# Splitting an attention block's end over three engines, and a bias as an extra weight row

## The chip, the cores and the metric

The kernel runs on one core of one Trainium2 chip, alone. The metric is the device time of one execution in microseconds (us), the median of several. A core has five engines with a queue of instructions each, which run in parallel and wait for each other by semaphores: TensorE (PE; weight loads are listed apart as PEld), VectorE (DVE), ScalarE (ACT), GpSimd (POOL) and SyncE (SP), which here only issues DMA transfers. Matmul results land in PSUM, everything else on the core lies in SBUF. All data is float32, and a float32 matmul appears in the trace as two matmul instructions.

## The reference

For each of four images x of 256 channels by 64 x 64 pixels (N = 4096 pixels), a self-attention layer is followed by a clustering layer with an MLP. The first one:

```python
q = einsum('oc,bcn->bno', wq, xf) + bq          # 32 channels
k = einsum('oc,bcn->bon', wk, xf) + bk[None, :, None]
attn = softmax(einsum('bnd,bdm->bnm', q, k), axis=-1)   # 4096 x 4096
v = einsum('oc,bcn->bon', wv, xf) + bv[None, :, None]
out = einsum('bcn,bmn->bcm', v, attn)
x = gamma[0] * out + x
```

The second layer, cut to what matters here, with the group norms taken over all channels and pixels of an image:

```python
y = x + ls1 * cluster(group_norm(x), ...)        # ends in conv1x1(out, proj_w, proj_b)
h = gelu(conv1x1(group_norm(y), mlp_w1, mlp_b1)) # 1024 channels
y = y + ls2 * conv1x1(h, mlp_w2, mlp_b2)
z = relu(batch_norm(y * dw_w)); out = relu(batch_norm(conv1x1(z, pw_w)))
```

## The kernel before, in words

The images are worked on one after the other, each in three stages: `attention`, `cluster`, `mlp`. An image lies in SBUF as four tiles of 1024 pixels (`xs`), is overwritten in place by the attention's result, and the next image's tiles are loaded while `mlp` frees them.

**Attention.** The 4096 query pixels are cut into 8 blocks of 512 (`nb`), the 4096 key pixels into 8 groups of 512 (`g`), so there are 64 units `u = 8*nb + g`. For one unit, `score` computes four 128x512 pieces of scores into two PSUM tiles (`sc`, halves of 128x1024; the pool `ps_s` has two such buffers, so the next unit's score can only start when both halves have been read), ScalarE copies them to an SBUF slot `s` (L282, L287; 10 slots), and VectorE keeps a running maximum `top` (L286, L289). After a block's eighth score, `fold` and `across` find the maximum of each query, and `spread` brings it into PSUM as `mb` by a matmul (L314). `exps` subtracts it on VectorE (L326), takes the exponential on ScalarE (L329) and sums on GpSimd into `acc` (L331 for the first group, then twice L334 a group; one `acc` buffer, so that the next block's first sum waits for the reading of the old one). `weigh` multiplies the exponentials with v into `av`, two PSUM tiles (L339, 16 matmul instructions a unit).

The scores run 9 units ahead of `weigh` (LEAD). The first nine scores are mixed with the computation of v (`v_pair`, L241; copies out of PSUM on VectorE and ScalarE in turn, L251 and L249). At a block's last unit, `finish` copies `av` times gamma into two tiles `t` (ScalarE L350, VectorE L351), computes the sum of the exponentials by matmuls with a matrix of ones (`den`, L354), takes its reciprocal (L356), multiplies (L358), adds gamma times v's bias and x (L360) and takes the statistics that the next group norm needs (bn_stats, L363).

**The order.** The program is written as above, and a scheduler then orders each engine's instructions by what they need. All 16 subtractions of a block, for example, come early in the block, as soon as `mb` is there, with the two maxima of each newer score between them. On the chip each engine takes its queue in this order.

**Cluster** starts with `group_norm` (bn_aggr of the statistics, two small matmuls with `mean_w`, square root, reciprocal), then projects, normalizes (L504: squares on GpSimd), finds for every pixel the best of four centers, and forms `gp`, the projected center values, by one matmul with `wproj_s` (96 rows) and one more that adds the projection bias by a row `row16` and `projb` (L600, L603). **MLP** runs per block of 512 pixels: 8 hidden tiles `hs` from the shared buffers with tag "w", the last convolution, and a DMA of the result.

At the start of the program, SP issues the loads in order; at most eight are under way, so that each later issue waits for the load eight before it. `projb` is made by a small matmul (L165) from `pc_s`.

## Time and profile before

| What | Value |
|---|---|
| Time, median of 3 | 4210.15 us (4208.2 to 4210.23) |
| Profiled execution, its own time | 4209.54 us |
| Its span | 4207.7 us |
| First score matmul | 38.98 us |
| First image: attention's blocks from den to den (block 0 to 6) | 156.11 to 639.87 us |
| First image: `den` of block 7 begins, bn_aggr begins | 696.51, 705.74 us |
| Granted TensorE clock, mean | 0.929 |

A page of the profile gives each engine's busy time and share, the chain of work that ended last (followed back from the last instruction), and groups of equal instructions with busy time, mean duration and the idle time of the engine just before them. An arrow `<-` names who ended a wait. "issue" is time in which nothing that the profile shows was waited for. Over the 40 slices of the span, TensorE and VectorE are busy like this (tenths):

```profile
PE   8998998799999899889999989988999989998899
...
DVE  4557655400456765540055675643005576564300
```

### The profile page before, as it was taken

The page shows a single profiled execution, that of the slowest core. Times are in us where ns is not written, and L with a number is a line of the kernel's source. Part 1 is how long each engine was busy: PE and PEld are TensorE (multiplying, and loading weights), DVE is VectorE, ACT ScalarE, POOL GpSimd, SP SyncE. Part 2 cuts the span into 40 slices and gives each one's busy share as a digit, 9 for nine tenths or more (in the row PEclk, how much of TensorE's full clock was granted, in tenths as well). Part 3 has the DMA queues.
Part 4 walks back from the last instruction along what each step waited for, and adds up shares of the span by engine and source line. Part 5 has one row for each costly group of instructions (what it writes and reads, how often), then busy time and mean ns, then how long its engine had stood idle before and what let it go on. Part 6 is the DMA issues. An engine that isn't in the chain of part 4 may idle for free.

```text
span 4207.7 us, 28649 instructions
## 1 busy us (share of the span) xinstructions
PE 3864.4 (92%) x11176; PEld 1736.7 (41%) x11176; DVE 1950.2 (46%) x1982; ACT 1471.3 (35%) x1723; POOL 1202.3 (29%) x526
## 2 busy tenths in 40 slices
PE   8998998799999899889999989988999989998899
PEld 4333334544433333444443333344444333335444
DVE  4557655400456765540055675643005576564300
ACT  5434432122634443212263443411226344341122
POOL 1534533000143553300024454340003345343000
PEclk9999999699999999969999999996999999998799
DMA  2000000010000000001000000000100000000000
GB/s 75 1 0 0 0 0 0 1 38 28 15 1 0 0 0 0 0 1 40 25 16 0 0 0 0 0 1 5 35 25 16 0 0 0 0 0 1 5 15 20
DMA packets 17639, 38.99 MB, mean 9 GB/s; under 512 B 2688, under 2 KB 4832, under 8 KB 17504
## 3 DMA queue, kind: packets, MB, share of 16 engines
q1 hardware_dynamic: 17504, 37.16, 2.5%
q8 instruction: 88, 1.44, 0.1%
q14 instruction: 47, 0.39, 0.0%
HBM read 20.38 MB, written 16.78 MB: 9 GB/s over the span
## 4 chain that ended last, share of the span: by engine, by line
PE 81%; DVE 16%; issue 2%; ACT 1%; DMA 0%; SPq 0%; DVEq 0%; ACTq 0%
PE av L339 37%; PE h L682 11%; PE mo L671 10%; PE sc L276 7%; DVE s L326 3%; DVE x L360 3%; PE pw L709 3%; PE vp L241 3%; DVE rden L356 2%; DVE t L358 2%; PE qp L256 2%; PE kp L220 1%; PE dots L510 1%; PE fp L436 1%; PE vp L448 1%
## 5 line engine op out<-in xcount | busy, mean ns | idle before, releaser
L339 PE MATMUL av<-s,v 128*128 128x512 f32 x4096 | 1877.7, 612 | 0.0
L339 PEld LDWEIGHTS av<-s,v 128*128 128x128 f32 x4096 | 780.7, 196 | 1076.4 <-issue 1054.2
L334 POOL TENSOR_TENSOR acc<-acc,s 128x1024 f32<-128x1024 f32 x448 | 1090.6, 2434 | 163.8 <-ACT s L329 130.8
L331 POOL TENSOR_TENSOR acc<-s 128x1024 f32<-128x1024 f32 x32 | 75.5, 2360 | 2207.6 <-ACT s L329 1168.5
L329 ACT ACTIVATE s<-s 128x1024 f32<-128x1024 f32 x512 | 532.0, 1056 | 444.6 <-DVE s L326 430.1
L326 DVE TENSOR_TENSOR s<-s,mb 128x1024 f32<-128x1024 f32 x512 | 591.1, 1210 | 36.2 <-PE mb L314 36.2
L286 DVE TENSOR_TENSOR top<-sc,top 128x1024 f32<-128x1024 f32 x224 | 272.1, 1215 | 677.4 <-PE sc L276 677.4
L276 PE MATMUL sc<-q,k 32*128 32x512 f32 x2048 | 356.2, 666 | 178.0 <-DVE top L289 171.2
L282 ACT COPY s<-sc 128x1024 f32<-128x1024 f32 x256 | 258.0, 1008 | 681.6 <-PE sc L276 681.6
L682 PE MATMUL h<-xn,w_s 128*128 128x512 f32 x1024 | 488.1, 601 | 8.3 <-DVE xn L656 6.2
L671 PE MATMUL mo<-hs,w_s 128*128 128x512 f32 x1024 | 476.1, 593 | 0.0
L698 DVE SCALAR_TENSOR_TENSOR x<-mo,pc_s,x 128x512 f32<-128x512 f32 x64 | 48.0, 751 | 918.5 <-PE mo L671 915.1
L690 ACT ACTIVATE hs<-h,pv_s 128x512 f32<-128x512 f32 x256 | 175.9, 687 | 579.2 <-PE h L682 577.0
L287 ACT COPY s<-sc 128x1024 f32<-128x1024 f32 x256 | 258.5, 1010 | 135.2 <-DVE top L286 93.6
L682 PEld LDWEIGHTS h<-xn,w_s 128*128 128x128 f32 x1024 | 197.5, 193 | 255.2 <-issue 253.2
L671 PEld LDWEIGHTS mo<-hs,w_s 128*128 128x128 f32 x1024 | 194.9, 190 | 244.8 <-issue 244.8
L289 DVE TENSOR_TENSOR top<-sc,top 128x1024 f32<-128x1024 f32 x224 | 273.4, 1220 | 17.9 <-DVE top L286 0.5
L276 PEld LDWEIGHTS sc<-q,k 32*128 32x128 f32 x2048 | 95.4, 190 | 384.8 <-DVE top L289 191.1
L360 DVE SCALAR_TENSOR_TENSOR x<-t,gbv,x 128x512 f32<-128x512 f32 x64 | 161.6, 2564 | 0.0
L709 PE MATMUL pw<-z,wpw_s 128*128 128x512 f32 x256 | 118.7, 607 | 3.3 <-ACT z L702 3.3
L241 PE MATMUL vp<-wv_s,x 128*128 128x256 f32 x512 | 119.1, 386 | 0.0
L284 DVE TENSOR_TENSOR top<-sc,s 128x1024 f32<-128x1024 f32 x32 | 39.2, 1224 | 158.6 <-ACT s L282 158.6
(143 smaller groups left out, 1972.8 us busy)
## 6 DMA issues: line engine op xcount, KB each, us to landing
x<-in_x SPq DMA_DIRECT2D x32, 512.0 KB, 4.8
out<-o SPq DMA_DIRECT2D x64, 256.0 KB, 2.0
w_s<-in_w SPq DMA_DIRECT2D x2, 1024.0 KB, 6.8
cst<-in_consts SPq DMA_DIRECT2D x1, 338.0 KB, 7.4
wqk_l<-in_wqk SPq DMA_DIRECT2D x1, 256.0 KB, 2.7
wv_s<-in_wv SPq DMA_DIRECT2D x1, 256.0 KB, 10.0
wpw_s<-in_wpw SPq DMA_DIRECT2D x1, 256.0 KB, 8.1
wfv_s<-in_wfv SPq DMA_DIRECT2D x1, 192.0 KB, 6.6
```

The lines of the kernel that those rows point to most:

```text
L276: nc.tensor.matmul(halves[r // 2][:, r % 2, :], k_s[rows, g, :], q_s[rows, :], start=True, stop=True)
L282: nc.scalar.copy(s[:, 0:2, :], halves[0])
L286: nc.vector.tensor_tensor(top, halves[1], top, ALU.max)
L287: nc.scalar.copy(s[:, 2:4, :], halves[1])
L289: nc.vector.tensor_tensor(top, halves[0], top, ALU.max)
L326: nc.vector.tensor_tensor(sh, sh, mxs[nb].unsqueeze(1).to_broadcast([P, 2, NB]), ALU.subtract)
L329: nc.scalar.activation(sh, sh, AF.Exp)
L334: nc.gpsimd.tensor_tensor(acc, acc, s[:, 2 * h : 2 * h + 2], ALU.add)
L339: nc.tensor.matmul(av[c], v_t[:, RG * g + quarter, c * P : (c + 1) * P], slots[u][:, quarter, :], start=(g == 0 and quarter == 0), stop=(g ...
L360: nc.vector.scalar_tensor_tensor(yb, ts[c], gbv[:, c : c + 1], yb, ALU.add, ALU.add)
L671: nc.tensor.matmul(acc[c], w2_s[:, j, c * P : (c + 1) * P], hs[j], start=(j == 0), stop=(j == HID // P - 1),)
L682: nc.tensor.matmul(ps[:, 0, :], w1_s[:, k, j * P : (j + 1) * P], xn[:, k, :], start=(k == 0), stop=(k == KC - 1),)
```

## The change: what it does

- **The block's end.** GpSimd first adds the two halves of `acc`, so `den` is one matmul. ScalarE copies `den` into SBUF. The reciprocal is taken there in four pieces of 128 columns, one in each of the next block's units 1 to 4, between `weigh`'s quarters. At unit 5, GpSimd multiplies both halves of `t` by it (128x1024) and adds them into x (128x1024). Unit 6 has nothing, and at unit 7 VectorE takes the statistics. After the last block the pieces run one after the other.
- **v's bias** is no longer added at the block's end. It is loaded into all partitions, and GpSimd adds it to v after ScalarE's copies (all of them now on ScalarE).
- **Projection bias:** `wproj_s` has a 97th row, loaded by a DMA of single values, and `agg` a 97th row with the ones; the second matmul of `gp`, `row16`, `projb` and the matmul that made it are gone.
- **Smaller:** `mean_w` is replaced by `ones` and a factor 1/128; the tag "w" has four buffers instead of five, shared by `dg`.

```diff
-    bv_s = loaded("bv_s", bv.rearrange("(k p o) -> p k o", p=P, o=1), [P, KC, 1])
+    bv_s = loaded("bv_s", bv.partition_broadcast(P), [P, C])
...
-    wproj_s = loaded("wproj_s", wproj, [ED, C])
+
+    wproj_s = const.tile([ED + 1, C], F32, name="wproj_s")
+    nc.sync.dma_start(out=wproj_s[:ED], in_=wproj)
+    ipb = PC.index("proj_b")
+    nc.sync.dma_start(out=wproj_s[ED:, :], in_=pc[:, ipb : ipb + 1].rearrange("c o -> o c"))
...
-    projb = const.tile([1, C], F32, name="projb")
-    pb_p = ps_m.tile([P, NB], F32, tag="m", name="pb_p")
-    for k in range(KC):
-        nc.tensor.matmul(
-            pb_p[:1, k * P : (k + 1) * P], par("proj_b", k), ident, start=True, stop=True
-        )
-    nc.vector.tensor_copy(projb, pb_p[:1, :C])
...
-            if i % 2:
-                nc.scalar.copy(v_t[:, 2 * i : 2 * i + 2, :], ps)
-            else:
-                nc.vector.tensor_copy(v_t[:, 2 * i : 2 * i + 2, :], ps)
+            pair = v_t[:, 2 * i : 2 * i + 2, :]
+            nc.scalar.copy(pair, ps)
+            nc.gpsimd.tensor_tensor(
+                pair, pair, bv_s.unsqueeze(1).to_broadcast([P, 2, C]), ALU.add
+            )
...
-            dg = work.tile([P, 4, P], F32, tag="dg", bufs=1, name=f"dg_{b}_{nb}")
+            dg = work.tile([P, 4, P], F32, tag="w", bufs=4, name=f"dg_{b}_{nb}")
...
         def finish(nb, av):
+
             acc = accs.pop(nb)
-            ts = [work.tile([P, NB], F32, tag="w", bufs=5, name=f"t_{b}_{nb}_{c}") for c in range(KC)]
-            nc.scalar.activation(ts[0], av[0], AF.Identity, scale=pvc("gamma"))
-            nc.vector.tensor_scalar(ts[1], av[1], pvc("gamma"), None, ALU.mult)
+            t_s = work.tile([P, KC, NB], F32, tag="t", bufs=1, name=f"t_{b}_{nb}")
+            nc.scalar.activation(t_s[:, 0], av[0], AF.Identity, scale=pvc("gamma"))
+            nc.vector.tensor_scalar(t_s[:, 1], av[1], pvc("gamma"), None, ALU.mult)
+            nc.gpsimd.tensor_tensor(acc[:, 0], acc[:, 0], acc[:, 1], ALU.add)
             den = ps_m.tile([P, NB], F32, tag="m", name=f"den_{b}_{nb}")
-            for t in range(2):
-                nc.tensor.matmul(den, ones, acc[:, t, :], start=(t == 0), stop=(t == 1))
+            nc.tensor.matmul(den, ones, acc[:, 0], start=True, stop=True)
             rden = work.tile([P, NB], F32, tag="rden", bufs=1, name=f"rden_{b}_{nb}")
-            nc.vector.reciprocal(rden, den)
-            for c in range(KC):
-                nc.vector.tensor_tensor(ts[c], ts[c], rden, ALU.mult)
-                yb = block(xs, c, nb)
-                nc.vector.scalar_tensor_tensor(
-                    yb, ts[c], gbv[:, c : c + 1], yb, ALU.add, ALU.add
-                )
-                nc.vector.bn_stats(stats[:, 2 * nb + c, :], yb)
+            nc.scalar.copy(rden, den)
+
+            def piece(i):
+                r = rden[:, i * P : (i + 1) * P]
+                nc.vector.reciprocal(r, r)
+
+            def last():
+                nc.gpsimd.tensor_tensor(
+                    t_s, t_s, rden.unsqueeze(1).to_broadcast([P, KC, NB]), ALU.mult
+                )
+                o = (nb % 2) * NB
+                yb = xs[nb // 2][:, :, o : o + NB]
+                nc.gpsimd.tensor_tensor(yb, yb, t_s, ALU.add)
+
+            def seen():
+                for c in range(KC):
+                    nc.vector.bn_stats(stats[:, 2 * nb + c, :], block(xs, c, nb))
+
+            return [lambda i=i: piece(i) for i in range(4)] + [last, lambda: None, seen]
...
             weigh(u, av, 1)
+            if g and later:
+                later.pop(0)()
             weigh(u, av, 2)
...
             if g == GRP - 1:
-                finish(nb, av)
+                later = finish(nb, av)
+        for piece in later:
+            piece()
         return stats
...
         agg = work.tile([P, 4, 32], F32, tag="q", name=f"aggs_{b}")
         nc.gpsimd.memset(agg, 0.0)
+        nc.gpsimd.memset(agg[ED : ED + 1, :, 16:17], 1.0)
...
         nc.tensor.matmul(
-            gp[:, :C], agg[:ED].rearrange("p q s -> p (q s)"), wproj_s, start=True, stop=False
-        )
-        nc.tensor.matmul(gp[:, :C], row16.rearrange("p q s -> p (q s)"), projb, start=False, stop=True)
+            gp[:, :C],
+            agg[: ED + 1].rearrange("p q s -> p (q s)"),
+            wproj_s,
+            start=True,
+            stop=True,
+        )
```

## The prediction

> **What bounds the kernel now.** I read the page first: busy times, the chain that ended last, the costliest groups.

> ```profile
> PE 3864.4 (92%) x11176; PEld 1736.7 (41%) x11176; DVE 1950.2 (46%) x1982; ACT 1471.3 (35%) x1723; POOL 1202.3 (29%) x526
> ...
> PE 81%; DVE 16%; issue 2%; ACT 1%; DMA 0%; SPq 0%; DVEq 0%; ACTq 0%
> ```

> TensorE sets the time except where VectorE does, for 16% of the span. The waits and groups say where:

> ```profile
> POOL acc L331 <- PE den L354: 1039.1, 28, 39.0
> ...
> PE sc L276 <- DVE top L289: 171.2, 24, 7.2
> ```

> ```profile
> L334 POOL TENSOR_TENSOR acc<-acc,s 128x1024 f32<-128x1024 f32 x448 | 1090.6, 2434 | 163.8 <-ACT s L329 130.8
> ...
> L360 DVE SCALAR_TENSOR_TENSOR x<-t,gbv,x 128x512 f32<-128x512 f32 x64 | 161.6, 2564 | 0.0
> ...
> L356 DVE RECIPROCAL rden<-den 128x512 f32<-128x512 f32 x32 | 107.2, 3351 | 3.9 <-PE den L354 3.9
> L358 DVE TENSOR_TENSOR t<-t,rden 128x512 f32<-128x512 f32 x64 | 101.3, 1625 | 0.4
> ...
> L331 POOL TENSOR_TENSOR acc<-s 128x1024 f32<-128x1024 f32 x32 | 75.5, 2360 | 2207.6 <-ACT s L329 1168.5 <-PE den L354 1039.1
> ```

> (Waits: us in total, times, longest. Groups: busy us, mean ns of one, idle before and its releasers.)

> There are 24 stalls of 7.1 us, six in each of four images: one after each block end (blocks 0 to 5) behind which scores still follow. GpSimd looks idle (29%), but its idle time is all of one kind: it waits about 37 us for `den` and then works without pause. The timeline of one block, all engines, shows it (start, duration):

> ```profile
> 399.89 1.88 PE L354 MATMUL den<-acc,ones 128*128 128x512 f32 x4
> ...
> 401.94 2.37 POOL L331 TENSOR_TENSOR acc<-s 128x1024 f32<-128x1024 f32 x1 [38.85 <-PE den L354]
> 402.46 3.35 DVE L356 RECIPROCAL rden<-den 128x512 f32<-128x512 f32 x1
> 404.39 10.79 POOL L334 TENSOR_TENSOR acc<-acc,s 128x1024 f32<-128x1024 f32 x4
> 410.16 5.57 DVE L360 SCALAR_TENSOR_TENSOR x<-t,gbv,x 128x512 f32<-128x512 f32 x2
> 418.11 2.08 PE L276 MATMUL sc<-q,k 32*128 32x512 f32 x4 [7.14 <-DVE top L289]
> 420.11 9.89 PE L339 MATMUL av<-s,v 128*128 128x512 f32 x16
> 420.41 24.32 POOL L334 TENSOR_TENSOR acc<-acc,s 128x1024 f32<-128x1024 f32 x10 [5.23 <-ACT s L329]
> ```

> After the wait a group of 16 `av` takes 9.89 us instead of 7.13. Over the six blocks of the first image the score and `av` after the stall take 2.2 to 3.8 us, on average 3.1, longer than an undisturbed step (8.13 us).

> [...] L360 takes 2.56 us on average, but 1.41 us for two in block 7, where GpSimd is idle. [...] I cost reciprocal pieces and bn_stats at their free durations. [...]

> **The change part by part.**

> *Block end on VectorE.* Out: 3.35 + 2×1.63 + 2×2.56 = 11.7 us in one lump. In: four pieces of 0.95 us (row L141, 128x128), spread out, and bn_stats later. So L289's lump is gone, and what is late next must be found. In the changed kernel's order of instructions each engine's queue after a block end reads:

> - GpSimd: first sum, ten additions (groups 1 to 5), scaling, addition into x, then groups 6 and 7.
> - VectorE: subtractions, reciprocals and the maxima of the next two scores, then all remaining subtractions, then the two bn_stats of this block, and only behind them the maxima of the third score.

> "Two steps later" is thus two steps in the program; the subtractions run ahead of it. bn_stats reads what GpSimd's addition into x wrote. The third score's maximum and second copy free the PSUM buffer that the fourth score needs (two buffers). So the new chain is: den, GpSimd 13 operations, bn_stats, maximum, copy, fourth score.

> I lay it on the times of the block above. `den` has two matmul instructions instead of four (like mb, 1.02 us), so it ends at 400.91; the new acc addition in front of it (half of 2.36 us) falls into GpSimd's 37 idle us. GpSimd starts at 401.1; first sum 2.37, gap 0.08, ten additions 24.3: 427.85. Their inputs are ready (the last exp near 416). Scaling and addition into x appear nowhere in the trace. They are two-SBUF-input operations of 128x1024 like L331 and L334, so I take 2.43 each (duration and gap): done 432.75. From below, L504 (a square, 96x1024) takes 1.87; from above, L334's longest is 2.9.

> VectorE meanwhile: five subtractions (1.15 each) to 400.8, gamma scaling 0.74, subtraction: 402.5; piece, subtraction, maximum 1.2, subtraction, maximum: 408.1. The second score's buffers are free before TensorE wants them at 409.0: the old stall is gone. Piece, two subtractions, piece, two subtractions, maximum, piece, maximum: 417.9, against a wish at 417.1: 0.8 us lost. Four subtractions: 422.4. There bn_stats waits 10.4 us for GpSimd, to 432.9. Then 1.2 (two bn_stats) + 1.2 (maximum) + 1.0 (copy) and hops: the fourth score starts at 436.45. TensorE was ready at about 426.1. It stands 10.3 us, more than the 7.1 removed, and is cold again.

> Compare at the same score. Before, it started at 438.07 with this block's 3.78 us of cold clock behind it; with the mean 3.13 it would be 437.4. Now 436.45 plus the cold 3.13 still to come: 439.6. So 2.2 us later a block; 24 × 2.2 = **+53 us**. The 0.86 us of the shorter `den` is in this.

> *Image end.* After block 7 nothing hides the pieces. Before: den starts 696.51, bn_aggr 705.74. Now: den to 697.5, ScalarE copy 0.6, four pieces 3.8, GpSimd 4.9, bn_stats 1.3 and hops: 708.3. 4 × 2.6 = **+10.4 us**. In block 7 no score follows, so bn_stats of block 6 holds nobody; its shorter `den` gives 4 × 0.86 = **−3.4 us**.

> *Projection bias as a 97th row.* One matmul pair less in a serial stretch (L603, two of 0.43): 4 × 0.86 = **−3.4 us**. Its new DMA of single values sits on SP's queue in front of w1, w2 and wpw, needed hundreds of us later: nothing. The memset on GpSimd sits where GpSimd idles 25 us.

> *Start.* TensorE's first instruction waited for pc_s (L165 <- DMA 18.3 us). That matmul is gone; the k blocks can start when x_0 has landed, about 9.0 us (the load eight issues on, waiting for it, issues at 8.96). k blocks at 3.7 us (first, cold), then 1.75; ScalarE now does five k blocks before the square roots that need pc_s and, by its order, loads a table there (1.28): the first score at about 29.6 instead of 38.98. **−9.4 us**; bounds −6 and −11. The larger bv_s (128 KB) goes ahead of pc_s, inside this.

> *v's bias.* All v copies go to ScalarE (one more of 0.58 in a step of 4.72 us, of which it uses 2.6), plus 16 GpSimd additions of about 1.2 in stretches where it idles: hidden. If the cover went, at most 16 × 0.6 = 10 us an image.

> *One answer, nothing:* four buffers for w (a slot's reader is at least two hidden tiles, about 7 us, ahead), ones instead of mean_w, dg in w's buffers.

> Sum: 53 + 10.4 − 3.4 − 3.4 − 9.4 = **+47 us**. Span 4207.7 gives 4254.9; the profiled execution took 4209.54, 1.8 more; so 4256.7, and with the median 0.6 above that execution **4257 us**.

> **The rivals.**

> *A, other side: GpSimd's pair is cheap.* 28 places (24 stalls, 4 image ends) pay for the pair, so it decides below 4.87 − 47/28 = 3.2 us; then no loss is left, and below 2.9 us it shows as faster. [...] For: one operand of the scaling is broadcast; L504 is quicker. Against: L331 and L334, the same engine and shape, never fell below 2.34. At L504's price (3.74) it is 4225, still slower.

> *B, dearer pair:* at 2.9 each, 28 × 0.95 more: 4283. The strided x operand speaks for it; the plain strides inside a row against.

> *C, bn_stats doesn't hold the scores, and TensorE runs through:* a block would take its 70 us of matmuls instead of 81.2: 24 × 11 = 265 less, near 3960. This needs GpSimd's addition done by VectorE's 422.4, each of 13 operations at 1.65 us instead of 2.43. Nothing shows that.

> **How the numbers follow.** The forecast 0.67 (own range 4240 to 4275: cold tails of 2.2 to 3.8 us, start −6 to −11); a pair near L504's price 0.11; B 0.12; A 0.09; C 0.01. Of A, half lies within 0.2% (about 8 us, what a measurement of this kernel can tell from no change). Faster 0.05, same 0.05, slower 0.90. The range 4222 to 4290 takes in L504's price and B.

> **What would show it.** After: VectorE's bn_stats waiting about 10 us, 24 times, for GpSimd's addition into x; TensorE's score waiting 10 us behind the third score's copy or maximum, 24 times, no longer 7.1 behind L289; the two new GpSimd rows near 2.4 us; the first score near 30 us; den to bn_aggr at image ends 2.6 us longer. Wrong if the new rows are under 1.6 us each, or the scores' wait is under 7 us.

## The result, and the profile after

The changed kernel takes 4222.53 us (median of 4, 4220.58 to 4223.4), the kernel before 4209.23 us (4 runs, 4208.2 to 4210.23). The ratio is 1.0031, 95% interval 1.0014 to 1.0048: slower, by 13.3 us, not by the 47 us forecast. The profiled span is 4221.0 us. It is read in the same order as before. First the page of the kernel after, busy times and the chain that ended last:

```profile
PE 3784.2 (90%) x11100; PEld 1709.7 (41%) x11100; DVE 1675.9 (40%) x1916; ACT 1518.6 (36%) x1788; POOL 1439.9 (34%) x687
...
PE 71%; POOL 13%; DVE 12%; ACT 2%; issue 2%; DMA 0%; POOLq 0%; SPq 0%; ACTq 0%; DVEq 0%
```

VectorE lost 274 us of work and GpSimd took on 238. The path did not get shorter by that: GpSimd, which had no share of the chain, now has 13% of it. The waits of the kernel after name who stands (us in total, times, longest), and the groups give the price of the new rows (busy us, mean ns of one, idle before and its releaser; a selection):

```profile
DVE st L360 <- POOL x L356: 347.8, 32, 15.4
...
PE sc L263 <- ACT s L274: 264.5, 28, 11.1
```

```profile
L348 DVE RECIPROCAL rden<-rden 128x128 f32<-128x128 f32 x128 | 119.1, 938 | 3.1 <-ACT rden L344 3.1
...
L351 POOL TENSOR_TENSOR t<-t,rden 128x1024 f32<-128x1024 f32 x32 | 74.9, 2340 | 70.9 <-DVE rden L348 70.9
L356 POOL TENSOR_TENSOR x<-x,t 128x1024 f32<-128x1024 f32 x32 | 74.8, 2339 | 2.2
L360 DVE BATCH_NORM_STATS2 st<-x 128x6 f32<-128x512 f32 x64 | 41.2, 686 | 347.8 <-POOL x L356 347.8
```

The 7.1 us stall behind the block end's lump is gone. In its place bn_stats waits for GpSimd after each block, and 24 scores wait 10.8 us behind it (the other four waits of that row come to 5 us together). The timeline of the kernel after, all engines, for the block end that the prediction was laid on:

```profile
392.75 1.02 PE L342 MATMUL den<-acc,ones 128*128 128x512 f32 x2
...
393.91 2.37 POOL L318 TENSOR_TENSOR acc<-s 128x1024 f32<-128x1024 f32 x1 [39.51 <-ACT s L316]
...
396.36 24.35 POOL L321 TENSOR_TENSOR acc<-acc,s 128x1024 f32<-128x1024 f32 x10
...
420.67 2.34 POOL L351 TENSOR_TENSOR t<-t,rden 128x1024 f32<-128x1024 f32 x1
...
423.09 2.34 POOL L356 TENSOR_TENSOR x<-x,t 128x1024 f32<-128x1024 f32 x1
...
425.46 1.29 DVE L360 BATCH_NORM_STATS2 st<-x 128x6 f32<-128x512 f32 x2 [11.09 <-POOL x L356]
...
426.67 1.21 DVE L273 TENSOR_TENSOR top<-sc,top 128x1024 f32<-128x1024 f32 x1
...
427.91 1.01 ACT L274 COPY s<-sc 128x1024 f32<-128x1024 f32 x1 [11.54 <-DVE top L273]
```

And what TensorE does when it is let go (TensorE's timeline of the kernel after):

```profile
428.97 2.36 PE L263 MATMUL sc<-q,k 32*128 32x512 f32 x8 [10.80 <-ACT s L274]
431.26 8.03 PE L326 MATMUL av<-s,v 128*128 128x512 f32 x16
439.13 1.88 PE L243 MATMUL qp<-x,wqk_s 128*128 128x512 f32 x4
440.94 1.14 PE L263 MATMUL sc<-q,k 32*128 32x512 f32 x8
442.01 7.13 PE L326 MATMUL av<-s,v 128*128 128x512 f32 x16
```

The chain is link for link the one forecast: `den`, first sum, ten additions, scaling, addition, bn_stats, maximum, copy, score. The score starts 428.97 − 392.75 = 36.2 us after `den`. What differs is the end: score and `av` after the wait take 439.13 − 428.97 = 10.16 us where an undisturbed step takes 8.14. Let the loss, here 2.0 us, be called the cold tail. Measured so at all 24 stalls it is 2.20 us on average after the change (1.85 to 2.77), and 3.04 us before it (2.06 to 3.69).

Laid side by side by stages (from one `den`, or one first instruction of a stage, to the next, summed over four images), the 13.3 us are:

| Stage | Forecast | Measured |
|---|---|---|
| Six block ends with scores behind them, 24 times | +53 | +24.3 |
| Image ends (`den` of block 7 to the group norm) | +10.4 | +8.6 |
| Shorter `den` inside block 7 | −3.4 | −3.4 |
| Cluster stage (97th row) | −3.4 | −8.0 |
| Start | −9.4 | −9.55 |
| k, v, first scores; MLP | 0 | +1.4 |
| Sum | +47 | +13.3 |

So the open questions were two: is the new chain really what the blocks pay for, and why is its price only half?

### The profile page after: what moved, and what is told of

The parts are those of the page before. It is cut to its first block, busy times and chain, and to the rows that moved or that the text cites. A ratio compares the mean times of both kernels' runs of the same rounds, so it can differ in the third digit from the quotient of the medians.

```text
span 4221.0 us, 28645 instructions
## 1 busy us (share of the span) xinstructions
PE 3784.2 (90%) x11100; PEld 1709.7 (41%) x11100; DVE 1675.9 (40%) x1916; ACT 1518.6 (36%) x1788; POOL 1439.9 (34%) x687
## 4 chain that ended last, share of the span: by engine, by line
PE 71%; POOL 13%; DVE 12%; ACT 2%; issue 2%; DMA 0%; POOLq 0%; SPq 0%; ACTq 0%; DVEq 0%
PE av L326 28%; PE h L689 11%; PE mo L678 10%; POOL acc L321 10%; PE sc L263 6%; DVE s L313 4%; PE pw L716 3%; PE vp L227 3%; POOL x L356 2%; POOL t L351 2%; PE qp L243 2%; PE fp L439 1%; PE kp L206 1%; PE dots L513 1%; PE vp L451 1%
## 5 line engine op out<-in xcount | busy, mean ns | idle before, releaser
L326 PE MATMUL av<-s,v 128*128 128x512 f32 x4096 | 1855.2, 605 | 0.0
L326 PEld LDWEIGHTS av<-s,v 128*128 128x128 f32 x4096 | 770.8, 193 | 1064.0 <-issue 1037.9
L321 POOL TENSOR_TENSOR acc<-acc,s 128x1024 f32<-128x1024 f32 x448 | 1058.0, 2362 | 32.6
L316 ACT ACTIVATE s<-s 128x1024 f32<-128x1024 f32 x512 | 541.0, 1058 | 194.7 <-DVE s L313 172.6
L263 PE MATMUL sc<-q,k 32*128 32x512 f32 x2048 | 333.4, 688 | 266.6 <-ACT s L274 264.5
L318 POOL TENSOR_TENSOR acc<-s 128x1024 f32<-128x1024 f32 x32 | 75.8, 2370 | 1097.6 <-ACT s L316 1097.6
L236 POOL TENSOR_TENSOR v<-v,bv_s 128x512 f32<-128x512 f32 x64 | 82.3, 1291 | 1035.9 <-ACT v L235 1034.5
L276 DVE TENSOR_TENSOR top<-sc,top 128x1024 f32<-128x1024 f32 x224 | 272.5, 1216 | 17.9 <-DVE top L273 0.5
L360 DVE BATCH_NORM_STATS2 st<-x 128x6 f32<-128x512 f32 x64 | 41.2, 686 | 347.8 <-POOL x L356 347.8
L348 DVE RECIPROCAL rden<-rden 128x128 f32<-128x128 f32 x128 | 119.1, 938 | 3.1 <-ACT rden L344 3.1
```

The source lines that it names most:

```text
L263: nc.tensor.matmul(halves[r // 2][:, r % 2, :], k_s[rows, g, :], q_s[rows, :], start=True, stop=True)
L276: nc.vector.tensor_tensor(top, halves[0], top, ALU.max)
L316: nc.scalar.activation(sh, sh, AF.Exp)
L321: nc.gpsimd.tensor_tensor(acc, acc, s[:, 2 * h : 2 * h + 2], ALU.add)
L326: nc.tensor.matmul(av[c], v_t[:, RG * g + quarter, c * P : (c + 1) * P], slots[u][:, quarter, :], start=(g == 0 and quarter == 0), stop=(g ...
```

## The experiments

### Is it bn_stats that holds the scores?

In VectorE's queue bn_stats stands ahead of the third score's maximum. Since the scheduler orders each queue by what the instructions need, another place in the program's text need not move it; a dependence does. Here a copy of 12 values a partition, out of the running maximum of the block two blocks on and into the slots that bn_stats then overwrites, puts it behind the `fold` (kernel e1_stats_tied):

```diff
+                    k = p // GRP - 2
+                    if k >= 0:
+                        nc.vector.tensor_copy(
+                            stats[:, 2 * k : 2 * k + 2, :], tops[p // GRP][:, :, :6]
+                        )
```

> The changed kernel with one tie added: a 12-element VectorE copy out of the maximum of the running score block into the statistics' place, so that bn_stats of block n stands behind all maxima of block n+2 in VectorE's queue. Theory (the fourth score waits for bn_stats, and bn_stats for GpSimd's two operations): the 10.8 us wait of TensorE goes at all 24 places, and with it the slow-clock tail of 2.1 us; VectorE reaches the third score's maxima at 414.4 on the changed kernel's times, before TensorE wants the fourth score; den to den falls from 82.0 to about 69 us, the span from 4221 to about 3910 us. Rival (GpSimd's longer queue holds the block elsewhere, at acc or at the score slots, or VectorE's added work does): a wait of several us shows up at another row and den to den stays above 75 us, the span above 4050 us.

Measured: 3901.46 us (3897.09 to 3904.27), ratio to the kernel before 0.9268 (0.9254 to 0.9282). Blocks take 68.95 us. The timeline of this kernel, all engines, where it used to stand:

```profile
407.71 0.17 DVE L395 COPY st<-top 128x12 f32<-128x12 f32 x1
407.98 1.29 DVE L360 BATCH_NORM_STATS2 st<-x 128x6 f32<-128x512 f32 x2
...
421.58 1.14 PE L263 MATMUL sc<-q,k 32*128 32x512 f32 x8
...
429.72 1.14 PE L263 MATMUL sc<-q,k 32*128 32x512 f32 x8
```

Here bn_stats runs without a wait, and the scores behind the block end come every 8.13 us, as in an undisturbed step; no score waits longer than 1.2 us any more. GpSimd's chain is as long as it was (32.7 us from `den` to the end of its addition into x, in both kernels); nobody on the path waits for it any more. That one place in a queue is worth 321 us: the change was good, and one instruction of it stood wrong.

### Which parts cost, which gain?

Two kernels take parts of the change alone. The first (e2_whole_recip) keeps GpSimd's part but takes the reciprocal whole, on VectorE:

```diff
-            nc.scalar.copy(rden, den)
+            nc.vector.reciprocal(rden, den)
...
-            return [lambda i=i: piece(i) for i in range(4)] + [last, lambda: None, seen]
+            return [last, lambda: None, seen]
```

> The changed kernel with the reciprocal in one piece straight from PSUM and no ScalarE copy. The scheduler then puts GpSimd's scaling and addition behind the first sum and three additions instead of ten, and bn_stats behind six fewer VectorE operations. Theory (the chain of GpSimd's queue up to bn_stats decides): addition into x ends about 16 us after den instead of 32.7, bn_stats waits about 3 us, the fourth score is free and only the third waits 3 to 5 us behind its predecessor's maximum; den to den about 75 to 77 us, the span about 4080 us (4060 to 4110). Rival (a whole 3.35 us reciprocal in VectorE's queue is what costs, and pieces are what helps): as slow as before or slower, den to den above 81 us, the span 4200 us or more.

Measured: 4053.14 us, ratio 0.9631 (0.9615 to 0.9647), span 4046.6, below the 4060 to 4110 expected; blocks 74.9 to 76.5 us, as expected. The scaling, no longer behind four pieces, stands in GpSimd's queue after three additions instead of ten. From the waits of this kernel:

```profile
DVE st L360 <- POOL x L356: 115.1, 32, 5.3
...
PE sc L263 <- ACT s L274: 77.1, 28, 3.3
```

The same two waits as in the changed kernel, a third as long. With the pieces, the chain of the changed kernel begins seven additions later.

The second (e3_other_parts) takes the block end of before (with v's bias left to GpSimd) and keeps everything else of the change:

```diff
-            nc.gpsimd.tensor_tensor(acc[:, 0], acc[:, 0], acc[:, 1], ALU.add)
...
+            nc.vector.reciprocal(rden, den)
+            for c in range(KC):
+                nc.vector.tensor_tensor(ts[c], ts[c], rden, ALU.mult)
+                yb = block(xs, c, nb)
+                nc.vector.tensor_tensor(yb, ts[c], yb, ALU.add)
+                nc.vector.bn_stats(stats[:, 2 * nb + c, :], yb)
...
-                later = finish(nb, av)
+                finish(nb, av)
```

> The other parts of the change alone: v's bias on GpSimd, the 97th row, ones for mean_w, four w buffers; the block end is that of before (without the bias in its last operation). Theory: the block ends are as before (den to den 80.2 to 81.8 us, 24 waits of 7.1 us), the start is 9.5 us shorter and each group norm to group norm stretch about 1.9 us: span about 4190 us. So the new block end costs about 30 us of 4221. Rival (the loss comes from the other parts, v copies on ScalarE for one): the span is 4205 us or more.

Measured: 4191.58 us, ratio 0.9959 (0.9944 to 0.9974), span 4191.1. So the other parts save 16.6 us of span and the new block end costs 4221.0 − 4191.1 = 29.9. The 7.2 us stall of the kernel before is back at its place.

### Why is the block end's price only half the forecast?

The cold tail was carried over as a fixed price of 3.13 us, and came out 0.9 us smaller. That the price is fixed was the author's assumption. The trace records the clock that TensorE was granted, as a share of full speed. Here it is around the stall shown above (stretch and its length in us; busy us and number of instructions of PE, PEld, DVE, ACT, POOL; then the granted clock, and two columns on DMA):

```profile
419.46:422.87 3.41, 0.00 (x0) 0.00 (x0) 0.00 (x0) 0.00 (x0) 3.41 (x2) 1.00 0.00 0
422.87:426.28 3.41, 0.00 (x0) 0.00 (x0) 0.82 (x2) 0.00 (x0) 3.33 (x3) 0.50 0.00 0
...
429.70:433.10 3.40, 3.40 (x10) 0.90 (x5) 1.61 (x2) 1.47 (x2) 3.24 (x3) 0.50 0.00 0
433.11:436.52 3.41, 3.41 (x9) 1.52 (x8) 0.82 (x1) 0.54 (x1) 3.20 (x2) 1.00 0.00 0
```

The clock falls to half at 422.87, 4.70 us after TensorE's last work ended, and is back at 433.11, 4.14 us after the score began. Half of 4.14 is 2.07, and the tail measured 2.0. In each of the eleven profiles the clock is only ever 1.00 or 0.50, and all its changes (83 in the kernel before, 81 in the changed one) lie on one grid of 3.4133 us, to within 0.01 us. The stretch from one point of this grid to the next is called a window here, and the point a boundary. In the seven kernels with waits of over 7 us in the blocks (168 of them), the tail is half of the time from the score's start to the clock's return, to within 0.12 us. That return is at the second or third boundary, 3.80 to 7.60 us after the start; what chooses between the two stays open. So at these stalls TensorE works at half speed until a boundary, and a stall that ends nearer to that boundary has less slow work to do: the first stall of image 1 in the changed kernel ends 5.64 us before it and has a tail of 2.77 us, the one above 4.14 us before it and has 2.0.

The blocks are drawn to whole windows by it. 24 windows are 81.92 us, and the blocks of the changed kernel in images 1 to 3 take 82.70, 82.31, 82.12, 82.02, 81.97 us, deviations of 0.78, 0.39, 0.20, 0.10, 0.05, each half of the one before. At half speed a start that is d later shortens the tail by d/2, so half of the lateness is left for the next block. Two experiments change the work in the chain and look whether the time follows.

The first (e4_half_scaling) shortens it by 1.1 us: GpSimd scales only the first half of the channels, so the second half stays unscaled.

```diff
-                    t_s, t_s, rden.unsqueeze(1).to_broadcast([P, KC, NB]), ALU.mult
+                    t_s[:, 0], t_s[:, 0], rden, ALU.mult
```

> The changed kernel with GpSimd's scaling done on the first half of the channels only (the other half stays unscaled): the chain from den to the fourth score is 1.1 us shorter at every block end. Theory (the slow clock after the wait ends at the boundary of a free-running window of 3.41 us, so den to den is drawn to 24 windows, 81.92 us, and a deviation halves from block to block): the score starts 1.1 us earlier, the tail is longer by as much, and den to den stays at 81.9 to 82.1 us from the third block on; only the four image ends gain, 4 us; the span is 4212 to 4217 us. Rival 1 (the tail has a fixed length): den to den 80.9, span about 4191 us. Rival 2 (the tail shortens with the length of the wait: 3.1 us after 7.1, 2.1 after 10.8): den to den about 81.2, span about 4198 us.

Measured, TensorE's timeline of this kernel at the same stall:

```profile
424.97 2.36 PE L263 MATMUL sc<-q,k 32*128 32x512 f32 x8 [9.70 <-ACT s L274]
427.26 9.08 PE L326 MATMUL av<-s,v 128*128 128x512 f32 x16
```

The wait is 1.1 us shorter (9.70 for 10.80), and the `av` behind it 1.05 us longer (9.08 for 8.03). Blocks take 81.91 to 81.96 us in images 1 to 3: the work taken out of the chain comes back as cold work. The kernel as a whole was a miss: 4194.96 us (4192.35 to 4195.06, ratio 0.9969, 0.9956 to 0.9982), well under what was expected, and its span, 4192.2 us, is near the 4191 of the first rival. The blocks, at 81.9 and not 80.9, speak against that rival; the rest is from the cluster stage, which took 99.05 us an image where the changed kernel takes 102.9, with the same instructions. That is taken up below.

The second (e5_one_more_pass) lengthens the chain by a whole pass of GpSimd, a multiplication with ones between scaling and addition:

```diff
+                t8 = t_s.rearrange("p k (a n) -> p (k a) n", n=P)
+                nc.gpsimd.tensor_tensor(
+                    t8, t8, ones.unsqueeze(1).to_broadcast([P, 8, P]), ALU.mult
+                )
```

> A third pass of GpSimd over 128x1024 (t times a tile of ones) between the scaling and the addition into x, about 2.34 + 0.08 = 2.42 us more in front of bn_stats. Theory (the cold clock ends only at a boundary of a running window of about 3.41 us, so den to den is drawn to whole windows): a block cannot stay at 24 windows, 81.92 us, since its cold tail would have to fall to -0.3 us; it goes to 25 windows, 85.3 us, with a cold tail of about 3.1 us instead of 2.1, that is 3.3 us more a block for 2.4 us of work. Rival 1 (the cold tail is a fixed price of a stall, 2.1 us): 82.0 + 2.4 = 84.4 us a block. Rival 2 (the tail shrinks further, the block stays near 82). Both stretches after block 7 (den to the group norm) 2.4 us longer: 14.5. Whole kernel: theory 24 x 3.3 + 4 x 2.4 = 89 more than the changed kernel, 4311; rival 1 68 more, 4290; the cluster stage may shift either by some 15 us.

Measured: the `den` matmuls of the first image in TensorE's timeline of this kernel:

```profile
146.70 1.02 PE L342 MATMUL den<-acc,ones 128*128 128x512 f32 x2
...
231.79 1.02 PE L342 MATMUL den<-acc,ones 128*128 128x512 f32 x2
...
317.00 1.02 PE L342 MATMUL den<-acc,ones 128*128 128x512 f32 x2
...
402.27 1.02 PE L342 MATMUL den<-acc,ones 128*128 128x512 f32 x2
...
487.58 1.02 PE L342 MATMUL den<-acc,ones 128*128 128x512 f32 x2
...
572.89 1.02 PE L342 MATMUL den<-acc,ones 128*128 128x512 f32 x2
```

From line to line 85.09, 85.21, 85.27, 85.31, 85.31: 25 windows are 85.33, and the deviation is halved again. The 2.4 us of work cost 3.3 us a block, since the tail grew to 3.0 us; the fixed tail would have given 84.4. The whole kernel, 4290.96 us (ratio 1.0193, 1.0176 to 1.021), equals what the rival gave, by chance: the blocks are as the theory had them and the cluster stage, at 98.95 us, gave 16 us back. The place decides, not the sum.

### Is the cluster stage, and so the whole image, drawn to windows too?

In the changed kernel the k blocks of images 1, 2 and 3 begin at 1063.19, 2114.53 and 3165.83 us: 1051.3 us apart, which is 308.0 windows. In the shorter chain they are 1044.5 apart (306.0), in the longer one 1068.4 (313.0). If the windows set the distance, then work added outside the blocks, in the serial stretch after block 7, must leave it a whole number too. Two kernels add a pass there, a whole one (e8_pass_at_image_end) and a half one (e9_half_pass_at_image_end):

```diff
+                if nb == NBLK - 1:
+                    t8 = t_s.rearrange("p k (a n) -> p (k a) n", n=P)
+                    nc.gpsimd.tensor_tensor(
+                        t8, t8, ones.unsqueeze(1).to_broadcast([P, 8, P]), ALU.mult
+                    )
```

(The half one takes `t8[:, :4]` and 4 in place of 8.)

> The changed kernel with one more GpSimd pass over 128x1024 (t times ones, about 2.42 us) only after block 7, where den, that pass and the group norm are one serial chain; the blocks are untouched. Den to the group norm 14.5 us instead of 12.1. Theory (each image's stalls end on boundaries of the same running window of 3.413 us, so one image to the next is a whole number of windows; in the changed kernel 1051.3 us = 308): from the k blocks of image 1 to those of image 2, and 2 to 3, the distance is again a whole number of windows to within 0.1 us: 1054.7 (309) or 1051.3 (308), or 1047.9 (307) if the cluster stage gets a kinder phase, but not 1053.7. Rival (durations add): 1053.7 us. Whole kernel: theory within -14 to +14 of the changed kernel's span of 4221.0, rival +10.

> As e8_pass_at_image_end with the pass over half as much (128x512, about 1.34 us): den to the group norm 13.4 us. Theory: image to image again a whole number of windows of 3.413 us (1051.3 = 308 or 1054.7 = 309, or 1047.9 = 307) to within 0.1 us, not 1052.6. Rival (durations add): 1052.6 us.

The first k matmuls of images 1, 2 and 3 in TensorE's timeline, first of the kernel with the whole pass, then of the one with the half pass:

```profile
1060.40 4.25 PE L206 MATMUL kp<-x,wqk_s 128*128 128x512 f32 x9
...
2111.73 8.65 PE L206 MATMUL kp<-x,wqk_s 128*128 128x512 f32 x19
...
3163.03 9.51 PE L206 MATMUL kp<-x,wqk_s 128*128 128x512 f32 x21
```

```profile
1057.56 6.82 PE L206 MATMUL kp<-x,wqk_s 128*128 128x512 f32 x15
...
2105.48 14.35 PE L206 MATMUL kp<-x,wqk_s 128*128 128x512 f32 x32
...
3153.38 14.35 PE L206 MATMUL kp<-x,wqk_s 128*128 128x512 f32 x32
```

1051.33 and 1051.30 us with 2.4 us more work (308 windows, as without it), and 1047.92 and 1047.90 us with 1.3 us more work: 307 windows, 3.4 us an image less than without the added work. `den` of block 7 to the group norm did get longer as computed, 14.53 and 13.45 us against 12.11. Whole kernels: 4221.5 us (4220.13 to 4222.61, ratio 1.0027, 1.0015 to 1.0039) and 4207.8 us (4206.67 to 4209.54, ratio 0.9997, 0.9987 to 1.0007). The second has more work than the changed kernel, waits for it on the path four times, and is 15 us faster. Where it is won is the cluster stage: 102.9 us in the changed kernel, 99.87 and 99.0 here. In it stand the 64 `nrm` matmuls, of 96x4 each:

```profile
741.51 11.70 PE L510 MATMUL nrm<-cst,sq 96*128 96x4 f32 x64
```

```profile
740.30 9.73 PE L515 MATMUL nrm<-cst,sq 96*128 96x4 f32 x64
```

```profile
739.58 9.22 PE L515 MATMUL nrm<-cst,sq 96*128 96x4 f32 x64
```

(TensorE's timelines of the changed kernel, the whole pass and the half pass.) The same matmuls after three different distances from the last block take 11.70, 9.73 and 9.22 us. The recorded clock says why: it falls to half inside this row, although TensorE has no gap there, 2.2 us after the first matmul in the changed kernel and 4.4 and 4.9 us after it in the other two. Before the fall a matmul starts every 111 ns, behind it every 213 ns. Over the whole stage the clock is at half for 65.4, 58.9 and 58.0 us (first image); half of the differences, 3.2 and 3.7 us, is about what the stage gained, 3.1 and 3.9 us. The stage gained what it no longer spent at half clock.

### Can the rest be had as well?

With bn_stats tied, two more kernels. One (e6_last_on_vector) gives block 7 its old ending on VectorE, since nothing hides GpSimd's passes there:

```diff
+            if nb == NBLK - 1:
+                nc.vector.reciprocal(rden, den)
+                for c in range(KC):
+                    yb = block(xs, c, nb)
+                    nc.vector.tensor_tensor(t_s[:, c], t_s[:, c], rden, ALU.mult)
+                    nc.vector.tensor_tensor(yb, t_s[:, c], yb, ALU.add)
+                    nc.vector.bn_stats(stats[:, 2 * nb + c, :], yb)
+                return []
```

> As e1_stats_tied, but block 7, behind which no score follows, ends as before the change: one reciprocal from PSUM, multiplication, addition and statistics on VectorE. Theory (after block 7 nothing hides ScalarE's copy, the four pieces and GpSimd's two passes): den to the group norm falls from 12.1 to about 9.8 us, blocks stay at 69.0 us, so 4 x 2.3 = 9 us less than e1_stats_tied: near 3892. Rival (the group norm waits for something else there): den to the group norm stays at 12.1, 3901. The cluster stage may vary by up to 3 us an image with the clock.

Measured: 3890.76 us (3883.31 to 3893.37), ratio 0.9241 (0.9227 to 0.9254), the fastest of all; near 3892 was expected. `den` to the group norm is 8.98 us, 3.1 less than 12.1 and not 2.3: the 9.8 expected was taken from a kernel whose `den` is 0.86 us longer. The median gains 10.7 us on the tied kernel. The profiled executions differ by 18 us in span (the one profiled here was the fastest of the four); 12.5 are from the image ends, about 5 from the stretches before the first `den` of each image, which take from 131.9 to 134.9 us in images 1 to 3 of the two kernels for the same work. Within this one kernel, too, the cluster stage takes 102.9, 99.9, 99.2 and 103.0 us in the four images, with the clock at half for 65.4, 58.9, 58.2 and 65.5 us.

The other (e7_tied_whole_recip) asks whether the pieces matter once bn_stats is tied: the tie, a whole reciprocal, GpSimd's part one unit later.

```diff
-            nc.scalar.copy(rden, den)
+            nc.vector.reciprocal(rden, den)
...
-            return [lambda i=i: piece(i) for i in range(4)] + [last, lambda: None, seen]
+            return [last] + 5 * [lambda: None] + [seen]
```

> As e1_stats_tied (statistics behind the fold in VectorE's queue), but the reciprocal in one piece of 3.35 us from PSUM, right after den, instead of a copy and four pieces, and GpSimd's scaling and addition one unit after the block's end. Theory (with bn_stats behind the fold, VectorE no longer holds the scores; the cut of the reciprocal matters only by the lump it puts ahead of the maxima, and 3.35 us are a fraction of the 11.7 us lump of the kernel before): 69 to 72 us a block, near 3900 to 3975. Rival (the pieces are what freed the scores, the lump stalls a score and costs a cold clock): over 74 us a block, over 4020.

Measured: 3919.93 us (3914.84 to 3920.55), ratio 0.931 (0.9296 to 0.9324), blocks 70.01 us, as expected. The copy and the pieces, with GpSimd's part at its later place, are worth 1.06 us a block (the three were not taken apart), and the two kernels are 18 us apart, beside the 321 of the tie.

## Why the prediction was wrong in size and right in direction

- **The chain and the queues: right.** 24 stalls, forecast 10.3 us behind bn_stats, measured 10.83 on average; the fourth score 36.25 us after `den`, forecast 36.56. The 0.8 us that the third score was to lose did not come: TensorE was ready that much earlier and waited that much longer. The old stall was gone, and the tied kernel showed that bn_stats alone held the scores.
- **GpSimd's pair: right.** Taken at 2.43 us each with the gap, measured 2.34 and a gap of 0.08. Rivals A (under 3.2 us for the pair) and B (5.8) fall with it: the scaling with its broadcast operand and the addition with its strided x took 2.34 us each, and the first sum (L318), which has neither, 2.37. (L504, from which a lower price was taken, runs 1.89 us by the trace, not 1.87.) That reciprocal pieces and bn_stats run no slower beside GpSimd was an assumption of the author's. In the changed kernel the pieces took 0.94 to 0.95 us beside it and 0.89 to 0.95 without it (0.95 taken), bn_stats 0.68 to 0.70 either way; in the kernel before, L360 took 2.82 us beside GpSimd and 0.75 where GpSimd did nothing. Rival C, that bn_stats holds nobody, was wrong for this kernel; its 70 us a block is nearly what the tied kernel reached (68.95). Its "near 3960" does not follow from its own terms: 4209 − 265, with image ends, `den`, row and start (−5.8), is about 3938.
- **The step that failed:** "now 436.45 plus the cold 3.13 still to come". The mean tail of the kernel before was put behind a stall that ends elsewhere in the window. It measured 2.20. (The tails before were also read some 0.09 us too long, 3.13 for 3.04, on both sides of the comparison.) With the score's start 0.31 us earlier that makes 2.2 − 0.93 − 0.31 = 0.96 a block, 24 × 0.96 = 23 us; the blocks measured +24.3 instead of +53. The recorded clock and the shorter and the longer chain showed that the tail is no price of a stall at all, but half of what is left to a window's boundary: 3.08, 2.20 and 3.01 us for three chains that differ only in the work in front. It should have been computed from the block's length: stall and full-speed work come to 80 us (82.17 less its tail of 2.22), and what that settles at is the next whole number of windows, 81.92 us, and not 83.1.
- **Image ends:** forecast +10.4, measured +8.6, right in kind. **Start:** −9.4, measured −9.55 at the first `den`, in part by luck: the k blocks began at 7.54 us and not at about 9.0, and from there to the first score (29.47 us; 38.91 before) it took 21.9 us where 20.6 were forecast. **The shorter `den`:** −3.4 both times.
- **The 97th row, mis-sized:** the removed pair is 0.69 us an image, forecast 0.86. The stage got 1.9 to 2.4 us shorter, the rest mostly in `tp` and the first `op` matmuls, which ran cold before and at full clock after (`tp` 1.70 and then 1.28 us). That is again the clock and not the row: in the first image of the kernel before the recorded clock was at half for 1.32 of the 1.70 us of `tp` and for all 2.09 us of the first eight `op` matmuls, in the changed one for none of either (1.28 and 1.14 us).
- **The edits costed at nothing** (v's bias, buffers, `ones`) show, if at all, in the +1.4 us of the table, which is −1.3 before the first `den` of images 1 to 3 and +2.7 in the MLP; which of them it was, or whether again the clock, was not tried.

## What to carry to other kernels

After moving work off a busy engine, look in the engines' queues for what waits for the moved work (here bn_stats, 348 us in all) and who stands behind it (here 24 scores, 10.8 us each); a dependence of 0.17 us that ties one instruction behind the urgent ones was worth more than all the rest, 321 us. Where TensorE stalls once per repetition as here, don't add durations to get the next time: add the full-speed work and the stall, and round up to whole clock windows of 3.413 us, as the blocks of 81.92 and 85.33 us did (a first estimate, good where what the rounding adds lies between the 1.9 and 3.7 us of cold tail seen here; the kernel before, with 78.0 us of work and stall, would need 0.5 us to 23 windows or 3.9 to 24, and settled on neither). And don't judge a change of a few microseconds by the total alone, since added work can come out faster (half a pass more, 15 us less); compare stage by stage.

## What the runs showed of the hardware

A TensorE without gaps lost its clock too: inside the row of 64 matmuls of 96x4 it fell to half in all 44 cases (four images of eleven kernels), 2.0 to 5.1 us after the first one. Whether the small size does it was not tried.

In the kernels without stalls in the blocks the distance of images is not always whole (965.91 us, 282.98 windows, and then 963.04, 282.14, in the fastest). In two of these three kernels the cluster stage varies by 3 to 4 us from image to image; in the third (e7_tied_whole_recip) it varies by 0.4.
